# Storing spectra in DRAM by channel and chunk, from SyncE's queue, with the first chunk in a store of its own

## The chip, the cores and the metric

The kernel runs on one core of a Trainium2 chip. The metric is the device time in microseconds (us) of one execution. The profile is of one execution on the chip. Its engines are PE (TensorE's matmuls), PEld (its weight loads), DVE (VectorE), ACT (ScalarE), POOL (GpSimd) and SP (SyncE, which only issues DMAs here). "L732" is line 732 of the kernel before.

## The reference, cut to what matters

A layer of neighbourhood attention and an MLP on four images of 56 x 56 pixels and 128 channels, then a second layer: a product with a global sum, and a spectral filter over the 3,136 tokens of each image.

```python
x = _L0_conv_ref(x, ...)                       # 7 x 7 neighbourhood attention, then an MLP
t = _to_tokens(x)                              # (4, 3136, 128)
t = t + _L1_attn_ref(_ln_t(t), ...)            # q * sum(k * v)
t = t + _L1_ffn_ref(_ln_t(t), ...)             # below
x = _from_tokens(t, x)

# _L1_ffn_ref, for each of four prefixes of the tokens, weighted and summed:
Vf   = rfft(phi, n); Uf_p = rfft(u, n); Uf_m = rfft(u * sgn, n)
out  = einsum('btkd,k,kde->bte', irfft(Vf * Uf_p), s, Mpp)
out += einsum('btkd,k,kde->bte', irfft(Vf * Uf_m) * sgn, s, Mpm)
out += sum over 3 lags of u shifted by the lag, times M_u[lag]
```

All that the change touches is how the spectra of `u` (the transform of the normalized tokens) pass through DRAM between the transform and the product with the filters.

## The kernel before, in words

**Stages.** The kernel has four stages in order of time. (1) Attention for images 0 to 3, in 28 steps an image; beside the steps of image b run the dense parts of image b-1 (`finish_image`: MLP, global sum, spectra) and the preparation of image b+1 (`start_image`, `keys`). A list of costs, the numbers that the generators yield, decides how many of these parts come after each attention step; up to `order.close()` the order of instructions on every engine is the one in which they are written. (2) After the last attention step, `finish_image(3)` alone, with the loading of the filter matrices into `mc` (`matrices`, L1015) ahead of its spectra. (3) The chunk loop, `for c in range(NCH)`, over 31 chunks of frequencies. (4) The way back to tokens.

**Spectra of an image** (`finish_image`, L686 to L734). The tokens of an image are in four pieces, j = 0 to 3, so with four images there are sixteen pieces. For each j and each of eight phases p, PE multiplies a `tab` tile of cosines and sines with transposed tokens into `px` (L708, 128 x 496). ACT, POOL and DVE add the eight `px` into the eight planes of `ab` (L716 to L730), a tile of 128 channels x 31 chunks x 8 planes x 16 values. When a j is complete, POOL's queue stores all of `ab` to `ud[j, b]` (L732): 128 rows, one per channel, of 31 x 512 = 15,872 bytes. In images 0 to 2 there is one `ab`; the sums of j+1 start from it and overwrite it in place (L729, L730), so DVE waits there until the store of j has landed. In image 3 two tiles alternate, so that j+2 waits for the store of j.

**What SP issues around it.** `waves` loads the `tab` tiles (L300): five tiles in images 0 to 2, so that four are ahead of the one in use, and ten in image 3. A new load waits until PE has used the tile whose place it takes. `residual(g)` fetches group g of the image two further on (L673, L99). SP's instructions run in the order written, and each waits for its own conditions.

**Chunks.** `fetch_tokens(c)` (L1036) loads the sixteen pieces of chunk c from `ud` into `xc`, a tile of 128 channels x 16 pieces x 128 values (512 bytes a piece). Chunk 0's load is cut in two, 12 pieces and 4, so that the first part need not wait for the last store. `tokens(c)` combines `xc` on POOL (chunk 0 on POOL and DVE) into `v`. `make(c, u)` multiplies filters `ph` with `mc` on PE into `pg` (L1088), and ACT and DVE copy it into `g` (L1104, L1106). `product(c, u)` multiplies `g` with `v` on PE into `py` (L1124), and the sums go to `yd` from SP (L1143). In the loop, PE alternates `make(c + 1, u)` and `product(c, u)`, 32 matmuls each, for u = 0 to 7. `tokens(c + 1)` is called at the top of chunk c; after `order.close()` the order is left to the scheduler, and SP issues a chunk's load two to three chunks before its product.

Of the kernel before, what the change touches and what calls it, by code (L numbers as in the profile page):

```python
# [9 lines left out]
FP = mybir.dt.float32  # L10
# [6 lines left out]
B, H, W, C = 4, 56, 56, 128  # L17
# [23 lines left out]
NP = 4  # L41
# [9 lines left out]
NCH = -(-R // FC)  # L51
SKIP = NCH * FC - R
FB = 4
CW = FC * PH * 2
# [6 lines left out]
def conv_attn_hybrid_kernel(ctx: ExitStack, tc: tile.TileContext, a: dict, out: bass.AP):  # L61
    nc = tc.nc

    cpool = ctx.enter_context(tc.tile_pool(name="const", bufs=1))
    dram = ctx.enter_context(tc.tile_pool(name="scratch", bufs=1, space=DRAM))
    xd = dram.tile([B, T, C], FP, name="xd")
    ud = dram.tile([NP, B, C, NCH * CW], FP, name="ud")
    pd = dram.tile([2 * NK, NCH * CW], FP, name="pd")

    yd = dram.tile([2, R, C + 8, C], FP, name="yd")  # L70
# [11 lines left out]
    def bank(name):  # L82
        return ps_s.tile([C, 512], FP, tag="s", name=name)
# [429 lines left out]
    def finish_image(b, own=None):  # L513
        x = xs[b]
# [161 lines left out]
        def last_steps(groups):  # L676
            for g in groups:
                recent(g)
                yield 2.3
                if g:  # L680
                    residual(g - 1)
                    yield 0.5
# [3 lines left out]
        ab = fp.tile([C, NCH, PH, 2 * FC], FP, tag="ab", name=f"ab_{b}")  # L686
        abs_of = (own.tile([C, NCH, PH, 2 * FC], FP, name="ab2") if own else ab, ab)
        for j in range(NP):
            before, ab = abs_of[(j + 1) % 2], abs_of[j % 2]
            toks = []  # L690
            for half in range(2):
                ps = ps_s.tile([L, 4, C], FP, tag="s", name=f"pt_{b}_{j}_{half}")
                for i in range(4):
                    at = off + N * j + PHASES[4 * half + i]
                    nc.tensor.matmul(
                        ps[:, i, :],
                        ut[:, at : at + PH * (L - 1) + 1 : PH],
                        ident,
                        is_transpose=True,
                        start=True,  # L700
                        stop=True,
                    )
                toks.append(fp.tile([L, 4, C], FP, tag="tok", name=f"tok_{b}_{j}_{half}", bufs=3))
                nc.scalar.copy(toks[half], ps)  # L704
                yield 0.4
            for i, p in enumerate(PHASES):
                ps = bank(f"px_{b}_{j}_{p}")[:, :RW]
                nc.tensor.matmul(ps, toks[i // 4][:, i % 4, :], next(tab), start=True, stop=True)  # L708
                src = ps.rearrange("c (g x) -> c g x", x=2 * FC)

                s, d = ab[:, :, p % 4], ab[:, :, 4 + p % 4]
                factor = ROOT if p % 2 else 1.0
                if p >= 4 and not (own and p == 6):
                    w = fp.tile([C, NCH, 2 * FC], FP, tag="tw", name=f"w_{b}_{j}_{p}", bufs=3)
                    nc.scalar.copy(w, src)  # L715
                    nc.gpsimd.tensor_tensor(s, s, w, ALU.add)  # L716
                    if p % 2:
                        w = fp.tile([C, NCH, 2 * FC], FP, tag="tw", name=f"wr_{b}_{j}_{p}", bufs=3)
                        nc.scalar.mul(w, src, factor)
                    nc.gpsimd.tensor_tensor(d, d, w, ALU.subtract)  # L720
                elif j == 0 and p < 4:
                    nc.scalar.copy(s, src)
                    nc.scalar.mul(d, src, factor)
                elif p >= 4:
                    nc.vector.tensor_tensor(s, s, src, ALU.add)
                    nc.vector.tensor_tensor(d, d, src, ALU.subtract)
                else:
                    s0, d0 = before[:, :, p % 4], before[:, :, 4 + p % 4]
                    nc.vector.tensor_tensor(s, s0, src, ALU.add)  # L729
                    nc.vector.scalar_tensor_tensor(d, src, factor, d0, ALU.mult, ALU.add)  # L730
                yield 0.85
            nc.gpsimd.dma_start(ud[j, b], ab.rearrange("c g p x -> c (g p x)"))  # L732
            if b < B - 1:
                yield from last_steps(range(2 * j, min(2 * j + 2, NG)))  # L734

# [199 lines left out]
    for b in range(B):  # L935

        def dense():
            if b == 0:
                setup_dense()
                yield 3.0  # L940
            yield from keys(b, 1)
            if b == 0:
                setup_gates()
                yield 0.0
                yield from filters()
            if b:
                yield "image"
                yield from finish_image(b - 1)
            if b + 1 < B:
                if b == 0:  # L950
                    fetch(b + 1)
                    yield "step"
                    yield "step"
                yield from start_image(b + 1)
                yield "keys"
                yield from keys(b + 1, 0)
# [79 lines left out]
    def fetch_tokens(c):  # L1036
        n = NP * B
        x = cp.tile([C, n, CW], FP, tag="xc", name=f"xc{c}")
        src = ud.rearrange("j b c w -> c (j b) w")[:, :, CW * c : CW * (c + 1)]

        for part in (slice(n),) if c else (slice(n - B), slice(n - B, n)):
            nc.sync.dma_start(x[:, part], src[:, part])
        fetched[c] = x

    def tokens(c):


        if c:
            fetch_tokens(c)
        n, x = NP * B, fetched.pop(c)  # L1050
        y = x.rearrange("c n (p r f) -> c p r n f", r=2, f=FC)
        gp = nc.gpsimd
        of, tag, bufs = [C, 3, 2, 2, n, FC], *(("od", 1) if c else ("v", 2))
        if c == 0:
            od = cp.tile(of, FP, tag=tag, name=f"od{c}", bufs=bufs)
        v = cp.tile([C, 3, n * FC, PH], FP, tag="v", name=f"v{c}")
        w = v[:, 1:].rearrange("c r k m -> c m r k")
        ev = cp.tile([C, 4, 2, n, FC], FP, tag="od", name=f"ev{c}", bufs=1)
        evens(gp if c else nc.vector, ev, y[:, :4], w[:, :4])
        if c:  # L1060
            od = cp.tile(of, FP, tag=tag, name=f"od{c}", bufs=bufs)
        odds(gp, od, y[:, 4:])
        od = od.rearrange("c i p r n f -> c i p r (n f)")
        gp.tensor_tensor(w[:, 4:6], od[:, 0], od[:, 2], ALU.add)
        gp.tensor_tensor(w[:, 6:], od[:, 0], od[:, 2], ALU.subtract)
        gp.tensor_scalar(v[:, 0], v[:, 2], -1.0, 1.0, ALU.mult, ALU.mult)
        spectra[c] = v
# [110 lines left out]
    with tc.tile_pool(name="last", bufs=1, side="right") as own, tc.tile_pool(  # L1178
        name="weigh", bufs=1, side="right"
    ) as wp:  # L1180
        extra, due, last = matrices(wp), 0.0, finish_image(B - 1, own)
        for spent in last:
            if spent == "spectra":
                break
            due += 0.45 * (spent if spent != "step" else 0.5)
            while due >= 1:
                next(extra, None)
                due -= 1
        run(extra)


    cp = chunks.enter_context(tc.tile_pool(name="w3", bufs=2, side="right"))
    filters_of(0)
    fetch_tokens(0)
    for n, _ in enumerate(last):
        if n == 2 * NG - 3:
# [29 lines left out]
    with tc.tile_pool(name="w4", bufs=1) as wp, tc.tile_pool(  # L1226
        name="ps_t", bufs=8, space=PSUM
# [232 lines left out]
```

## Time and profile before

| what | value |
|---|---|
| runs of the kernel | 1994.88, 1998.28, 2002.96 us; median 1998.28 |
| profiled execution, its own time | 2011.3 us |
| its span, first to last instruction | 2009.5 us |
| mean granted TensorE clock | 0.966 |
| busy share of the span: PE, PEld, DVE, ACT, POOL | 94%, 60%, 60%, 51%, 45% |
| DMA moved | 223.44 MB in 183,406 packets |
| `ud` <- `ab` (L732) | 16 DMAs of 1,984 KB on POOL's queue, 8.5 us from issue to landing (median) |
| `xc` <- `ud` (L1042) | 30 DMAs of 1,024 KB, one of 768 KB, one of 256 KB, on SP's queue |

The profiled execution was some 13 us slower than the median of the runs; durations below come from it. A group's line names the line of code, the engine, the operation and its tiles, "output<-inputs". A wait is put down to the instruction that released it; "issue" means that the engine waited for nothing that the profile shows. The chain of waits follows the work that ended last back from the end of the span: 77% of it is PE, 8% issue, 6% DVE and 4% DMA.

### The profile page before, as it was taken

To read this page: it belongs to the slowest core of one execution; us is meant where nothing else is said; L and a number is where in the kernel's file an instruction comes from. 1 tells how busy PE (TensorE), PEld (TensorE's weight loads), DVE (VectorE), ACT (ScalarE), POOL (GpSimd) and SP (SyncE) were. 2 spreads that over 40 slices of the span, in tenths; PEclk is the share of its full clock that TensorE was granted. 3 is DMA by queue.
4 is the path that set the end of the run, shared out by engine and by line. 5 is a ranking of instruction groups with operands and counts; after the bars stand their busy time and mean duration, and the time that the engine had idled before them with its cause. 6 is when DMAs were issued, how large, how long until landed. Compare 5 with 4: busy or idle time off the path is not lost.

```text
span 2009.5 us, 57128 instructions
## 1 busy us (share of the span) xinstructions
PE 1881.9 (94%) x23926; PEld 1206.8 (60%) x23926; DVE 1204.3 (60%) x2749; ACT 1024.2 (51%) x2311; POOL 904.1 (45%) x1441
## 2 busy tenths in 40 slices
PE   6899999999999999999999998999999999996998
PEld 3555555565555555555565445888888888883333
DVE  3666635455544556445555765677676666674983
ACT  2566685655685656775555342555555555550000
POOL 2344321474322465222472036777877787760000
PEclk8799999899999999998999999999999999998999
DMA  4040000153000252000244539344444444439981
GB/s 114 22 141 12 1 1 1 28 193 131 1 1 1 85 189 79 1 1 1 94 157 176 189 105 308 91 123 124 129 125 113 121 132 116 115 105 386 353 317 64
DMA packets 183406, 223.44 MB, mean 111 GB/s; under 512 B 11576, under 2 KB 160121, under 8 KB 180556
## 3 DMA queue, kind: packets, MB, share of 16 engines
q1 hardware_dynamic: 169712, 160.53, 26.5%
q0 software_dynamic: 2352, 33.01, 4.1%
q10 hardware_dynamic: 11084, 26.24, 3.7%
q8 instruction: 189, 3.10, 0.6%
q14 instruction: 69, 0.57, 0.1%
HBM read 141.77 MB, written 77.97 MB: 109 GB/s over the span
## 4 chain that ended last, share of the span: by engine, by line
PE 77%; issue 8%; DVE 6%; DMA 4%; ACT 3%; POOL 2%; ACTq 0%; SPq 0%; DVEq 0%; POOLq 0%
PE pg L1088 14%; PE py L1124 13%; PE pi L1272 7%; PE px L708 5%; PE ppt L817 4%; PE pl L761 4%; PE ph L551 3%; PE pf L542 3%; PE par L644 3%; PE pav L874 2%; PE pv L837 2%; PE pk L483 2%; ACT p L788 1%; DVE p L774 1%; DMA ud<-ab 1%
## 5 line engine op out<-in xcount | busy, mean ns | idle before, releaser
L801 POOL TENSOR_SCALAR p<-p,den 112x280 f32<-112x280 f32 x448 | 216.2, 502 | 491.2 <-DVE den L799 254.3
L1106 DVE COPY g<-pg 128x512 f32<-128x512 f32 (+1 forms) x496 | 320.3, 691 | 171.2 <-PE pg L1088 171.1
L1104 ACT COPY g<-pg 128x512 f32<-128x512 f32 (+1 forms) x496 | 263.9, 584 | 236.8 <-PE pg L1088 236.8
L1088 PE MATMUL pg<-ph,mc 32*128 32x128 f32 x7936 | 300.4, 284 | 6.5 <-DVE g L1106 5.2
L1124 PE MATMUL py<-g,v 128*32 128x128 f32 x7840 | 283.0, 281 | 12.6 <-issue 12.2
L1088 PEld LDWEIGHTS pg<-ph,mc 32*128 32x128 f32 x7936 | 251.8, 187 | 48.1 <-issue 38.3
L788 ACT ACTIVATE p<-p,low 112x280 f32<-112x280 f32 x448 | 231.2, 517 | 91.9 <-DVE low L774 91.5
L1124 PEld LDWEIGHTS py<-g,v 128*32 128x32 f32 x7840 | 222.5, 152 | 46.8 <-issue 18.1
L774 DVE CUSTOM_DVE_ANT_0 p<-pl,bias 112x280 f32<-112x280 f32 x448 | 174.8, 446 | 15.9 <-PE pl L761 4.1
L824 DVE COPY pt<-ppt 120x448 f32<-120x448 f32 x112 | 69.4, 620 | 111.2 <-PE ppt L817 110.4
L817 PEld LDWEIGHTS ppt<-ident,p 112*120 112x120 f32 x896 | 100.4, 139 | 57.7 <-issue 40.1
L817 PE MATMUL ppt<-ident,p 112*120 112x112 f32 x896 | 127.3, 263 | 5.5 <-DVE middle L859 4.1
L708 PE MATMUL px<-tab,tok 98*128 98x496 f32 x256 | 118.1, 607 | 12.6 <-ACT tok L704 9.8
L716 POOL TENSOR_TENSOR ab<-ab,w 128x496 f32<-128x496 f32 x60 | 74.5, 1242 | 101.9 <-ACT w L715 58.3
L824 ACT COPY pt<-ppt 120x448 f32<-120x448 f32 x224 | 87.2, 444 | 56.3 <-PE ppt L817 56.2
L551 PE MATMUL ph<-ln_m,w_fc 128*128 128x448 f32 x224 | 103.8, 555 | 4.7 <-DVE ln_m L532 4.7
L761 PE MATMUL pl<-kt,qt 32*112 32x280 f32 x896 | 95.7, 444 | 11.6 <-ACT qt L502 6.0
L559 ACT ACTIVATE h<-ph,b_fc 128x448 f32<-128x448 f32 x112 | 69.4, 633 | 61.8 <-PE ph L551 60.3
L542 PE MATMUL pf<-h,w_fc 128*128 128x448 f32 x224 | 100.8, 540 | 0.0
L318 POOL TENSOR_TENSOR v<-ev 128x512 f32<-128x512 f32 x30 | 39.6, 1320 | 120.1 <-PE py L1124 120.0
L708 PEld LDWEIGHTS px<-tab,tok 98*128 98x128 f32 x256 | 48.2, 197 | 65.8 <-issue 41.5
L564 DVE SCALAR_TENSOR_TENSOR x<-pf,b_fc,x 128x448 f32<-128x448 f32 x28 | 19.1, 684 | 113.0 <-PE pf L542 113.0
(239 smaller groups left out, 3401.6 us busy)
## 6 DMA issues: line engine op xcount, KB each, us to landing
ring<-yd SPq DMA_DIRECT2D x64, 512.0 KB
ud<-ab POOLq DMA_DIRECT2D x16, 1984.0 KB, 8.5
xc<-ud SPq DMA_DIRECT2D x30, 1024.0 KB
tab<-in_tab SPq DMA_DIRECT2D x160, 189.9 KB
yd<-ys SPq DMA_DIRECT2D x118, 256.0 KB
mat<-in_M_phi_plus SPq DMA_DIRECT2D x16, 512.0 KB
mat<-in_M_phi_minus SPq DMA_DIRECT2D x16, 512.0 KB
x<-in_x SPq DMA_DIRECT2D x28, 224.0 KB
```

Source lines behind the costliest of these rows:

```text
L542: nc.tensor.matmul(po[:, :GT], late["w_fc2"][:, i, :], hts[g - 1][i], start=(i == 0), stop=(i == 3),)
L551: nc.tensor.matmul(ph[:, :GT], w_fc1[:, i * C : (i + 1) * C], lnm[:, g * GT : (g + 1) * GT], start=True, stop=True,)
L708: nc.tensor.matmul(ps, toks[i // 4][:, i % 4, :], next(tab), start=True, stop=True)
L761: nc.tensor.matmul(pls[h][:TQ, :KEYS], qts[b, g][hs, t * TQ : (t + 1) * TQ], kt[hs, r0 : r0 + KR, c0 : c0 + KC], start=True, stop=True,)
L774: nc.vector.tensor_tensor_reduce(out=f["p"][:, h, :], in0=f["pls"][h][:TQ, :KEYS], in1=bias[:, h, :], scale=-1.0, scalar=3.0e38, op0=ALU.a ...
L788: nc.scalar.activation(f["p"][:, h, :], f["p"][:, h, :], AF.Exp, bias=f["low"][:, h : h + 1], scale=-1.0, accum_out=f["den"][:, h : h + 1],)
L801: nc.gpsimd.tensor_scalar(f["p"][:, h, :], f["p"][:, h, :], f["den"][:, h : h + 1], 1.0, ALU.mult, ALU.mult)
L817: nc.tensor.transpose(ppt[:, i, :], of, ident[:TQ, :TQ])
L1088: nc.tensor.matmul(banks[rg][:, q, :], mc[r, 4 * u + q, :], t[r, at : at + CW], start=True, stop=True,)
L1104: nc.scalar.copy(into, src)
L1106: nc.vector.tensor_copy(into, src)
L1124: nc.tensor.matmul(py[32 * m : 32 * m + 32, f - f0, :], weights(v, 1 - r, f, slot), g[:, (2 * slot + r) * FC + f, :], start=(r == 0), stop ...
```

## The change

`ud` gets another layout. Before, a row was a channel of one piece, with all 31 chunks side by side. After, a row is a channel of all pieces: chunks 1 to 30 follow one another, and within a chunk its sixteen pieces lie side by side, 8,192 bytes together. Each row is followed by 1,024 unused values. Chunk 0 lies in a store of its own, `ud0`, one row of 8,192 bytes per channel.

The store of each j and image becomes two DMAs, both on SP's queue instead of POOL's: 128 pieces of 512 bytes to `ud0`, and 128 x 30 pieces of 512 bytes to `ud`. In SP's order they stand where the store is written, after the `tab` loads of that j and before what SP loads next. The load of a chunk becomes 128 rows of 8,192 bytes; chunk 0's is still cut in two (6,144 and 2,048 bytes a row) and reads `ud0` alone. In the built program the order of instructions on PE and DVE is the same as before, POOL's lacks the sixteen stores, four `ph` loads on ACT's queue stand a few instructions apart, and SP has the 32 stores; the rest is unchanged.

```diff
-    ud = dram.tile([NP, B, C, NCH * CW], FP, name="ud")
+    ud0 = dram.tile([C, NP * B, CW], FP, name="ud0")
+    ud = dram.tile([C, (NCH - 1) * NP * B * CW + 1024], FP, name="ud")
+    ud_of = ud[:, : (NCH - 1) * NP * B * CW].rearrange("c (g n w) -> c g n w", g=NCH - 1, w=CW)
...
-            nc.gpsimd.dma_start(ud[j, b], ab.rearrange("c g p x -> c (g p x)"))
+            spectrum = ab.rearrange("c g p x -> c g (p x)")
+            nc.sync.dma_start(ud0[:, B * j + b], spectrum[:, 0])
+            nc.sync.dma_start(ud_of[:, :, B * j + b], spectrum[:, 1:])
...
     def fetch_tokens(c):
         n = NP * B
         x = cp.tile([C, n, CW], FP, tag="xc", name=f"xc{c}")
-        src = ud.rearrange("j b c w -> c (j b) w")[:, :, CW * c : CW * (c + 1)]
+        src = ud_of[:, c - 1] if c else ud0
 
         for part in (slice(n),) if c else (slice(n - B), slice(n - B, n)):
             nc.sync.dma_start(x[:, part], src[:, part])
```

## The prediction

> **What bounds the kernel now.** I read the profile in this order: busy time by stage, the chain of work that ended last, then the stages that touch `ud`, instruction by instruction. The first view is busy time of the engines in stretches of the span. Its columns are the stretch, its length, the busy us of PE, PEld, DVE, ACT and POOL with instruction counts, then the granted clock, the DMA share and GB/s. The three lines are the spectra of image 0 beside attention, the last image's spectra, and the chunk loop.
> ```profile
> 380.00:475.00 95.00, 90.77 (x637) 56.90 (x637) 51.96 (x165) 53.82 (x145) 64.04 (x89) 0.96 0.47 159
> 1190.00:1247.00 57.00, 52.93 (x191) 30.56 (x189) 25.00 (x42) 22.45 (x43) 34.11 (x33) 0.97 0.83 282
> 1272.00:1808.00 536.00, 523.73 (x15069) 451.22 (x15064) 372.61 (x589) 287.47 (x530) 400.45 (x547) 1.00 0.44 119
> ```
> PE is the bound of the chunk loop (524 of 536 us), with POOL at 400 and DMA at 0.44. So the chunk loads can only matter where they make PE wait. They do. The timeline of one chunk (start, length, engine and line; idle time and its end in brackets):
> ```profile
> 1501.87 0.36 SPq L1042 DMA_DIRECT2D xc<-ud  x1
> ...
> 1505.61 1.12 PE L1124 MATMUL py<-g,v 128*32 128x128 f32 x32
> ...
> 1507.85 0.99 PE L1124 MATMUL py<-g,v 128*32 128x128 f32 x25
> ...
> 1509.53 0.47 PE L1124 MATMUL py<-g,v 128*32 128x128 f32 x7 [0.69 <-issue]
> ```
> PE stops in the middle of 32 like matmuls and waits for no other engine ("issue"). The same stretch in slices of 1 us:
> ```profile
> 1503.00:1504.00 1.00, 1.00 (x40) 0.88 (x36) 0.46 (x1) 0.42 (x1) 0.92 (x3) 1.00 0.49 131
> 1504.00:1505.00 1.00, 1.00 (x40) 0.83 (x35) 1.00 (x3) 0.66 (x2) 1.00 (x2) 1.00 1.11 336
> ...
> 1507.00:1508.00 1.00, 1.00 (x36) 0.88 (x34) 0.44 (x2) 0.10 (x1) 1.00 (x2) 1.00 1.08 311
> 1508.00:1509.00 1.00, 0.84 (x25) 0.59 (x23) 1.00 (x2) 0.97 (x2) 1.00 (x2) 1.00 0.59 166
> 1509.00:1510.00 1.00, 0.47 (x11) 0.32 (x11) 0.15 (x1) 0.00 (x0) 1.00 (x3) 1.00 0.07 21
> ```
> The load has the DMA engines full from about 1503 to 1508, and PE starves right after. What is missing is instructions, which the page's list of DMA queues shows to come by DMA too:
> ```profile
> q8 instruction: 189, 3.10, 0.6%
> ```
> That is packets, MB and share; 16,384 bytes a packet. In the trace's packet records these start about every 4 us, except the one that falls on a load: in the chunks from 1285 on it starts 4.5 to 5.2 us after the load's issue, when the load's last pieces have gone (1506.94 here, after 1500.15).
>
> Last, who waits for the stores: the waits around `ud`, and two lines of DVE's timeline in the last image.
> ```profile
> DVE ab L729: 17.1, 5
> ...
> DMA to landing us min/median/max: 6.6/8.5/10.4
> ```
> ```profile
> 1211.27 0.67 DVE L729 TENSOR_TENSOR ab<-ab,px 128x496 f32<-128x496 f32 x1 [2.20 <-DMA ud<-ab]
> ...
> 1221.79 0.67 DVE L729 TENSOR_TENSOR ab<-ab,px 128x496 f32<-128x496 f32 x1 [4.12 <-DMA ud<-ab]
> ```
> DVE may overwrite `ab` only when the store that reads it has landed, so a later landing is late work for DVE.
>
> **What the Trainium skill says.** "Runtime: NRT & Kernel Launch", Instruction fetch mechanics: instructions are refilled in 16 KiB blocks of 256 through a DMA queue of their own, and the cost of a block is "mostly hidden". The trace agrees on the size; hidden it is not here (0.69 us above). "DMA: Bandwidth & Descriptors", Queues, rings and completion order: a DMA engine changes queues only at packet boundaries, at most 64 descriptors. Here the fetch waited for all 128 pieces an engine had of the load, so the wait is at least as long as that says. Same page, Two DMAs through the same engine are not ordered: transfers of one queue start in order. So what SP issues after a store starts after its pieces. Same page, Latency and other measured facts: a row pitch of a large power of two slows DRAM, and 4 KiB of padding restores it. The new pitch, (30 x 16 x 128 + 1024) x 4 = 249,856 bytes, is such a padded one; no run here shows its effect, and I take no penalty.
>
> **The change, part by part.**
> *Loads (L1042).* Now 2,048 pieces of 512 bytes, 128 per engine. The packet records give 27 ns for such a piece: 3.5 us, which with 1.0 us to the first piece ends near 4.6 us after issue, as seen. After: 128 rows of 8,192 bytes, 8 per engine. This size is not in the trace; between 6,272 bytes (239 ns) and 12,544 (476 ns) on a hardware queue lies 311 ns, so 2.5 us, ending at 3.5 us. The fetch can start some 1.2 us sooner. What it is worth: loads are issued at 1284.92 and, 26 chunks on, at 1760.07, so 18.28 us a chunk. Eight undisturbed pairs of 32 `pg` and 32 `py` matmuls, 2.157 us each (1731.17 to 1733.33), are 17.25. The excess is 1.03 x 26 = 26.7 us, nearly all in the one pair after the load (3.51 us at 1727.66, 2.59 in the chunk of 1303). No such stall is much over 1.35, so 1.2 us removes nearly all: I take **24 us off**, for 27 chunks. Bounds: 0 (the wait has another cause) and 28 (all excess gone). Below zero is not excluded by the trace, as 8 KB pieces might hold an engine longer; I give that no weight of its own, since the bytes and their total time shrink.
>
> *Stores.* Sixteen DMAs of 128 rows on POOL's queue become 32 on SP's, of 128 and 3,840 pieces. POOL sheds 16 x 0.6 us; PE paces that stage, so I count nothing. Drain before: 8 x 595 ns = 4.8 us if alone. After: 240 x 27 ns = 6.5 us; 38 ns, the 95th percentile, would be 9.1. From POOL's last operation on `ab`, landing before: 0.3 + 6.6/8.5/10.4 = 6.9/8.8/10.7, the slow ones beside `tab` and `x` loads on the other queue. After: 0.45 for the small store's issue, 1.0 to the first piece, 6.5, and 0.6 to the release (sem to DVE as before) = 8.6, and no later transfer of SP's competes. So +0.5 us on a mean. It gates DVE nine times in images 0 to 2 (three turns each); attention's work lies beside it, so I count half: 9 x 0.25 = **+2.3 us**.
>
> *What SP has behind the stores.* SP now waits for POOL, and behind stand `tab` loads (L300), `x` loads (L99) and, at the end, `ph` and `xc`. In images 0 to 2 the `tab` loads needed next are already issued. But the `x` loads of groups 5 and 6 after the fourth store are due at once: PE multiplies them (L390) from 478.93. They land near 481.4 behind a store that starts at 473.7 and drains by 480.2, against about 479.8 needed: +1.6 us, for images 2 and 3, **+3.2 us**.
>
> *Last image.* POOL ends the first store's data at 1202.5. Store pieces run 1204 to 1210.5, landing 1211.3, as before (1211.27). The first `tab` load behind it, due at 1210.5, lands near 1211.8: PE +1.3. The next store's pieces follow seven or eight `tab` loads (0.58 us each at 168 packets a us) and land near 1222, as before; the `tab` behind lands at 1222.5, and PE ends this stage **1.7 us late**. Chunk 0's loads stand behind the fourth large store, but read smaller pieces and wait for the small stores alone: landed near 1243.5, against 1244.2 now, and DVE turns to them only after 1245.8. Nothing gained, nothing lost; without that cover each us would cost one.
>
> **Sum:** -24 + 2.3 + 3.2 + 1.7 = -17 us. The profiled execution took 2011.3 us (span 2009.5 and 1.8 around it), so 1994. It lies 13 us above the median of the runs, 1998.28; I carry the difference over: **1981**.
>
> **The rivals.** *A: the loads are not what holds the fetch*, or an engine's eight large pieces hold it as long, or rows are cut into short pieces after all (the change not doing what it says; 12,544-byte packets in the trace speak against). The stall stays, the costs stay: 1998 + 7 = 2005. For it: the size of packet is new. Against: the fetch starts with the load's end in every chunk.
> *B: slower.* The store's 512-byte pieces written 8 KB apart go slower than 27 ns, and SP's queue hands the delay on. Each us of drain costs about 9 x 0.5 for DVE, 2 for `x` loads and 3 for the last image, 9.5 us; so 17 us are gone at 1.8 us more drain, 35 ns a piece. At 45 ns (+4.3 us, 41 us) it gives 1981 + 41 = 2022. For: contended pieces took 38 ns. Against: the `yd` stores, also 512-byte pieces, take 27 to 34 ns.
>
> **Chances.** Forecast 0.66, A 0.20, B 0.14. Half a per cent, 10 us, is about what can be told from no change. The forecast's own range is 1970 (all 28 us, no cost) to 1991 (20 us gained, 13 lost), a little of it within 10 us; A lies within; B mostly beyond. So faster 0.64, same 0.23, slower 0.13. The range reaches to A's time: 1970 to 2004.
>
> **What will show it.** Right: chunk loads 17.3 to 17.4 us apart, no "issue" gap of PE after them, the fetch about 3.6 us after issue. L729's waits for `ud` near 17 us or a few more; PE's `px` in the last image waiting for `tab` once or twice for 1 to 2 us. Wrong: chunks still at 18.2 (A), or stores landing over 10 us after POOL's last operation and PE's px waiting for it (B).

## The result and the profile after

The changed kernel is slower, not faster: 2022.2 us (median of 4 runs, 2013.2 to 2028.0) against 1996.6 us for the kernel before beside it, ratio 1.012 (95% interval 1.0073 to 1.0167). Measured once more (experiment 12) it is 1.0137 (1.0108 to 1.0166). The forecast was 1981, range 1970 to 2004. The profiled execution took 2020.1 us with a span of 2018.3. After the change a line from `finish_image` on has a number higher by 4 to 6: L729 is now L733, L732 is L737 (small store) and L738 (large store), L1042 is L1048, L1088 is L1094, L1124 is L1130.

First the busy time by stage, image 0's spectra, the last image's, and the chunk loop; the second and third stretch are moved to where these stages now lie. The first is not, though image 0's first store stands 9.3 us earlier in it than before.
```profile
380.00:475.00 95.00, 86.67 (x576) 52.90 (x574) 44.14 (x140) 50.69 (x134) 59.76 (x81) 0.95 0.53 149
1212.00:1270.00 58.00, 53.19 (x176) 29.27 (x175) 23.31 (x39) 21.54 (x41) 29.14 (x24) 0.94 0.83 243
1301.00:1837.00 536.00, 522.57 (x15296) 453.80 (x15296) 377.97 (x596) 288.08 (x531) 400.92 (x548) 0.99 0.43 131
```
The loop does what was forecast: in 536 us PE now gets through 15,296 matmuls, before 15,069. In image 0's spectra PE gets through 576 in 95 us (580 when the stretch is moved by 9 us), before 637, and its busy time falls from 90.8 to 86.7 us.

The gain first. The timeline of one chunk (start, length, engine and line) around its load:
```profile
1523.00 0.33 SPq L1048 DMA_DIRECT2D xc<-ud  x1
1523.49 1.17 PE L1094 MATMUL pg<-ph,mc 32*128 32x128 f32 x32
1524.60 1.12 PE L1130 MATMUL py<-g,v 128*32 128x128 f32 x32
1525.65 1.17 PE L1094 MATMUL pg<-ph,mc 32*128 32x128 f32 x32
1526.75 1.12 PE L1130 MATMUL py<-g,v 128*32 128x128 f32 x32
1527.81 1.25 PE L1094 MATMUL pg<-ph,mc 32*128 32x128 f32 x32
1528.98 1.12 PE L1130 MATMUL py<-g,v 128*32 128x128 f32 x32
```
The 32 matmuls run through, without the "issue" gap. Loads are issued at 1313.3 and, 26 chunks on, at 1769.3: 17.54 us a chunk, before 18.28.

Then the loss. The timeline of image 0 at its first store, SP's queue and what waits on DVE:
```profile
394.06 1.22 POOL L724 TENSOR_TENSOR ab<-ab,wr 128x496 f32<-128x496 f32 x1
...
395.31 0.35 SPq L737 DMA_DIRECT2D ud<-ab  x1
...
395.71 0.43 SPq L738 DMA_DIRECT2D ud<-ab  x1
...
396.18 4.77 SPq L103 DMA_DIRECT2D x<-in_x  x1
...
401.05 12.26 SPq L304 DMA_DIRECT2D tab<-in_tab  x8
...
404.98 0.67 DVE L733 TENSOR_TENSOR ab<-ab,px 128x496 f32<-128x496 f32 x1 [5.49 <-DMA ud<-ab]
...
406.38 0.73 PE L767 MATMUL pl<-kt,qt 32*112 32x280 f32 x4 [0.32 <-DVE ab L734]
```
DVE may write `ab` 9.7 us after POOL's last operation on it (395.28). It stands idle for 5.49 us, and attention's own next matmul (`pl`) waits 0.32 us for it; longer waits follow. In the kernel before, the same write came 7.6 us after POOL's last operation (404.34), and `px`, not the store, released it:
```profile
411.92 0.67 DVE L729 TENSOR_TENSOR ab<-ab,px 128x496 f32<-128x496 f32 x1 [3.21 <-PE px L708]
```
SP's next issue after the large store takes 4.77 us in place of 0.3 to 0.4. Who waited for `ud`, in total and times:
```profile
  DVE ab L733: 37.3, 8
  POOL od L327: 19.0, 1
  DVE ev L316: 2.8, 1
```
Before, DVE waited 17.1 us in five places and POOL 13.4 us once. The chain of waits now runs through the DMAs of image 0 (start, length, what; most of it left out):
```profile
395.71 9.15 DMA ud<-ab
...
418.18 10.29 DMA ud<-ab
...
452.49 7.51 DMA tab<-in_tab
...
480.47 5.58 DMA x<-in_x
486.09 1.86 PE xm_a L394 x2
```
The store itself is on it twice, then a `tab` load and an `x` load that stand behind a store.

The two traces by stretch, cut at store and load issues (the stretch up to the first store, which the change doesn't touch, is 9.3 us shorter in the changed kernel's profiled execution; I leave it out). A *turn* is the time from one store of an image to its next.

| stretch | before, us | after, us | difference |
|---|---|---|---|
| nine turns, images 0 to 2 | 206.0 | 229.2 | +23.2 |
| fourth store to the first of the next image, three times | 592.5 | 599.9 | +7.4 |
| last image, first to fourth store | 27.4 | 30.8 | +3.4 |
| fourth store to the load of chunk 4 | 54.7 | 58.1 | +3.4 |
| 26 chunks | 475.2 | 456.0 | -19.2 |

### The profile page after: what moved, and what is told of

It is laid out like the page before. It is cut to its first block, busy times and chain, and to the rows that moved or that the text cites. A ratio compares the mean times of both kernels' runs of the same rounds, so it can differ in the third digit from the quotient of the medians.

```text
span 2018.3 us, 57154 instructions
## 1 busy us (share of the span) xinstructions
PE 1881.7 (93%) x23926; PEld 1205.6 (60%) x23926; DVE 1201.7 (60%) x2749; ACT 1023.4 (51%) x2311; POOL 893.3 (44%) x1425
## 3 DMA queue, kind: packets, MB, share of 16 engines
q1 hardware_dynamic: 174320, 193.03, 30.7%
## 4 chain that ended last, share of the span: by engine, by line
PE 72%; DMA 8%; issue 7%; DVE 6%; ACT 3%; POOL 2%; SPq 0%; ACTq 0%; DVEq 0%; POOLq 0%
PE pg L1094 14%; PE py L1130 13%; PE pi L1278 7%; PE ppt L823 4%; PE px L712 4%; PE pl L767 3%; PE ph L555 3%; PE pf L546 3%; DMA ud<-ab 3%; PE pav L880 2%; PE pv L843 2%; PE par L648 2%; DVE p L780 2%; PE pk L487 1%; DMA tab<-in_tab 1%
## 5 line engine op out<-in xcount | busy, mean ns | idle before, releaser
L1094 PE MATMUL pg<-ph,mc 32*128 32x128 f32 x7936 | 297.5, 284 | 8.2 <-DVE g L1112 8.1
L1130 PE MATMUL py<-g,v 128*32 128x128 f32 x7840 | 278.1, 281 | 3.0 <-issue 2.5
L1094 PEld LDWEIGHTS pg<-ph,mc 32*128 32x128 f32 x7936 | 249.8, 187 | 48.6 <-issue 36.2
L1130 PEld LDWEIGHTS py<-g,v 128*32 128x32 f32 x7840 | 220.9, 152 | 34.0 <-issue 5.2
L712 PE MATMUL px<-tab,tok 98*128 98x496 f32 x256 | 123.9, 628 | 18.6 <-ACT tok L708 10.1
L880 PE MATMUL pav<-pt,v 120*32 120x112 f32 x1792 | 88.0, 268 | 0.0
```

The lines of the kernel that those rows point to most:

```text
L1094: nc.tensor.matmul(banks[rg][:, q, :], mc[r, 4 * u + q, :], t[r, at : at + CW], start=True, stop=True,)
L1130: nc.tensor.matmul(py[32 * m : 32 * m + 32, f - f0, :], weights(v, 1 - r, f, slot), g[:, (2 * slot + r) * FC + f, :], start=(r == 0), stop ...
```

## The experiments

**Theory:** the loop has its gain, and the loss is the later landing of stores in short pieces, which holds DVE at `ab`, with loads behind them as a second term. **Rivals:** SP's queue order alone costs it; or short pieces cost by themselves wherever they stand. Each ratio is to the kernel before, timed beside it. In the table below, *gate* is the mean time from POOL's last operation on `ab` to DVE's next write of it, over nine turns, whether the store or `px` ends it; *next* is the sum of the three stretches to the next image.

| kernel | ratio, 95% | gate, us | nine turns | next | us a chunk |
|---|---|---|---|---|---|
| before (its profile) | 1 | 9.3 | 206.0 | 592.5 | 18.28 |
| changed (its profile) | 1.012 (1.007-1.017) | 11.1 | 229.2 | 599.9 | 17.54 |
| 1 only the loads | 0.986 (0.984-0.989) | 9.4 | 205.1 | 589.2 | 17.51 |
| 2 old rows, SP stores | 1.004 (1.002-1.005) | 8.7 | 203.6 | 591.1 | 18.34 |
| 3 new layout, POOL stores | 1.021 (1.018-1.024) | 14.0 | 261.3 | 588.5 | 17.60 |
| 4 new layout, ACT stores | 1.020 (1.017-1.023) | 11.4 | 224.6 | 617.3 | 17.54 |
| 5 x loads first | 1.007 (1.005-1.010) | 11.0 | 227.1 | 584.8 | 17.53 |
| 6 old rows, stored twice | 1.048 (1.046-1.051) | 13.8 | 262.6 | 613.9 | 18.08 |
| 7 load in four | 0.989 (0.987-0.991) | 9.1 | 204.5 | 586.9 | 17.52 |
| 8 load in two | 0.999 (0.997-1.000) | 9.3 | 203.9 | 588.5 | 18.25 |
| 9 load in eight | 0.989 (0.986-0.991) | 9.4 | 204.9 | 586.2 | 17.38 |
| 10 half the store | 0.986 (0.984-0.988) | 8.5 | 202.2 | 586.0 | 17.57 |
| 11 no pad | 1.017 (1.014-1.019) | 11.5 | 236.4 | 600.7 | 17.56 |
| 12 changed, again | 1.014 (1.011-1.017) | 11.1 | 230.8 | 601.4 | 17.55 |
| 13 x loads first, again | 1.009 (1.006-1.012) | 11.0 | 228.5 | 586.6 | 17.54 |
| 14 no pad, again | 1.015 (1.012-1.018) | 11.4 | 233.0 | 599.8 | 17.51 |

**1. Only the loads change.** The kernel before with
```diff
-        src = ud.rearrange("j b c w -> c (j b) w")[:, :, CW * c : CW * (c + 1)]
+        src = ud[c % NP, c // NP % B, :, : NP * B * CW].rearrange("c (n w) -> c n w", w=CW)
```


> The kernel before, with one thing changed: each chunk's load reads 128 rows of 8,192 bytes side by side out of the old store's layout (the numbers in them are another chunk's, so the output is not the reference's); layout and queue of the stores stay. Theory (chunk loop gains, spectra lose): chunk loads 17.5 us apart in place of 18.28, so 26 x 0.75 = 19 to 20 us faster than before, ratio about 0.990, and the spectra of images 0 to 3 as in the kernel before. Rival (the shorter interval hangs on the new store too, for example on its padded pitch): interval stays near 18.2, ratio 0.998 to 1.002.


Measured 0.986, chunks 17.51 us apart. The loop's gain is real and needs nothing of the new stores. (The ratio holds a few us that are not the loop's: chunk 0's load no longer reads the last store, and POOL waits for it 9.0 us in place of 13.4.)

**2. The store of before, from SP.** `nc.gpsimd.dma_start(ud[j, b], ...)` becomes `nc.sync.dma_start`.


> The kernel before, with its store of 128 rows of 15,872 bytes issued by SyncE in place of GpSimd; layout and chunk loads stay. Theory (the loss comes from 3,968 pieces a store, which fill SP's queue, so that the loads behind are issued 5 to 7 us late and DVE's ab comes free later): 128 rows drain in 4.8 us and don't block SP, so at most 0 to 8 us slower, ratio 1.000 to 1.004. Rival (it is the order on SP alone: tab and x loads stand behind a store that waits for POOL, whatever its pieces): 20 us or more slower, ratio 1.010 or more.


Measured 1.004. So the queue's order alone is not the loss: the nine turns are 2 us shorter than before, since rows on SP land a little sooner. What it costs lies at the end, in the last image (31.3 us against 27.4) and ahead of the loop. DVE hardly waits for the stores here:
```profile
  DVE ab L729: 6.9, 2
```

**3 and 4. The new layout from other queues.** Both stores with `nc.gpsimd` or `nc.scalar` in place of `nc.sync`.


> The changed kernel, with both stores of a spectrum issued by GpSimd (software queue) as before the change; layout and chunk loads as changed. Theory (half of the loss is loads behind the store on SP, half the later landing): tab and x loads are issued on time again, the landing stays at 10 us or more after POOL's last operation, DVE still waits over 35 us for ab; chunk loop 17.5 us a chunk; 10 to 20 us faster than the changed kernel, ratio to before 1.000 to 1.005. Rival (pieces alone cost it, wherever they are issued): 2015 to 2025 us, ratio 1.010 or more; GpSimd may also spend long on writing 4,096 descriptors, which would show as POOL idle time after each store.

> The changed kernel, with both stores issued by ScalarE on its own hardware queue in place of SyncE; layout and chunk loads as changed. Theory (loads behind the store on SP): SP issues tab and x loads on time (0.4 us an issue, not 4.8), PE's xm_a of groups 5 and 6 runs through; but ACT now waits for POOL's last operation at each store, with evictions behind it, 1 to 5 us each; net 0 to 15 us faster than the changed kernel, ratio to before 1.003 to 1.012. Rival (landing alone): no difference to the changed kernel beyond 5 us, or slower by ACT's waits.


Both miss: 1.021 and 1.020, slower than from SP. Neither queue helps. From POOL the `x` and `tab` loads are on time ("next" 588.5), but the pieces land later still, POOL's two issues take 0.6 and 1.6 us, and DVE waits twice as long as in the changed kernel:
```profile
  DVE ab L733: 77.1, 10
```
The turns are 55 us longer than before for it. From ACT DVE waits for the stores only 16.9 us, in four places; the gate of 11.4 is long because in the third turn of each image (13.5 to 14.2 us) `px` ends it, which comes late behind ACT. The turns are 5 us shorter than from SP, but "next" is 25 us longer than before, and the last image takes 42.7 us in place of 27.4. Here ACT's own next DMA issue is held behind the store, and its copies and squares for PE stand behind that issue:
```profile
473.05 0.36 ACTq L737 DMA_DIRECT2D ud<-ab  x1
473.46 1.06 ACTq L738 DMA_DIRECT2D ud<-ab  x1
474.62 0.58 ACT L673 COPY xf<-pf 112x512 f32<-112x512 f32 x1 [4.75 <-POOL p L807]
477.04 5.02 ACTq L674 DMA_DIRECT2D xd<-xf  x1
...
482.15 0.58 ACT L673 COPY xf<-pf 112x512 f32<-112x512 f32 x1 [6.95 <-PE xm_a L394]
...
482.79 1.02 PE L394 MATMUL xm_a<-x,center 128*128 128x448 f32 x2 [0.96 <-ACT xf L673]
```
The last copy is put down to PE's `xm_a`, but ACT had been busy issuing until 482.06. So the expectation that half of the loss goes once the stores leave SP's queue was wrong: to ACT the held issue moves with the store, and from POOL the landing is later still. The two do show the terms apart. From POOL, with no load of SP held, the turns alone are longer; from ACT, with shorter waits at `ab`, most of the loss lies outside the turns.

**6. Landing alone.** The kernel before with SP's rows of 15,872 bytes stored twice, the second time to a scratch `ud2`.
```diff
-            nc.gpsimd.dma_start(ud[j, b], ab.rearrange("c g p x -> c (g p x)"))
+            nc.sync.dma_start(ud[j, b], ab.rearrange("c g p x -> c (g p x)"))
+            nc.sync.dma_start(ud2[j, b], ab.rearrange("c g p x -> c (g p x)"))
```


> The kernel before, with the store of 128 rows of 15,872 bytes issued by SyncE, and issued a second time into a scratch of its own: no short pieces, but DVE gets ab back only when 256 rows have gone, 4.8 us later. Theory (what costs is the landing that gates DVE, not the number of pieces): DVE's first write to ab comes 12 to 15 us after POOL's last operation in place of 7.5 to 10, each turn between stores is 5 to 8 us longer, 15 to 20 us an image, some 45 to 60 us in all, ratio to before 1.025 to 1.035. Rival (short pieces cost by themselves, through SP's blocked issue or held instruction fetches, and half of a later landing is hidden by attention as the prediction had it): 1.010 to 1.015.


Measured 1.048, more than expected, with not one short piece in the stores. The nine turns are 59 us longer than in experiment 2. PE waits 22.8 us for DVE's writes of `ab`, and the loads behind the second store come late too: 11.6 us for `x` and 16.0 for `tab`, part of it within the turns. In this timeline SP's next issue is hardly held (0.86 us), and DVE is:
```profile
399.18 0.35 SPq L733 DMA_DIRECT2D ud<-ab  x1
399.58 0.43 SPq L734 DMA_DIRECT2D ud<-ab  x1
400.11 0.86 SPq L100 DMA_DIRECT2D x<-in_x  x1
...
411.92 0.67 DVE L730 TENSOR_TENSOR ab<-ab,px 128x496 f32<-128x496 f32 x1 [8.56 <-DMA ud<-ab]
```
So a late landing costs without short pieces and without SP's slow issue. Here some late `tab` loads are mixed in; in experiment 3 PE waits for none in images 0 to 2. The two together show the first term.

**10. Half the pieces.** The changed kernel storing 15 of the 30 chunks in `ud`, and reading them twice.
```diff
-            nc.sync.dma_start(ud_of[:, :, B * j + b], spectrum[:, 1:])
+            nc.sync.dma_start(ud_of[:, :15, B * j + b], spectrum[:, 1:16])
-        src = ud_of[:, c - 1] if c else ud0
+        src = ud_of[:, (c - 1) % 15] if c else ud0
```


> The changed kernel, storing only chunks 1 to 15 beside chunk 0 (1,920 short pieces in the large store in place of 3,840) and reading those twice over for chunks 16 to 30, so that the output is not the reference's. Queue, layout, pieces and all 27 loads of the loop stay. Theory (landing gates DVE): the large store lands some 4 us sooner, DVE's first write comes 6 to 8 us after POOL's last operation, turns are back at 68 us an image, loads behind the store are 4 us less late; only the chunk loop's gain of 20 us is left, ratio 0.989 to 0.993. Rival (short pieces on SyncE cost by themselves: blocked issue, held fetches): half of the loss stays, ratio 0.998 to 1.004.


Measured 0.986, better than expected. With the same layout, queue and kind of piece, but the last piece 5.6 us after issue in place of 10.4, the whole loss is gone: DVE no longer appears among those who wait for `ud`, and it finds `ab` free when its `px` is there. SP's next issue takes 0.71 us here, so this run takes away both terms:
```profile
402.10 0.35 SPq L737 DMA_DIRECT2D ud<-ab  x1
402.51 0.43 SPq L738 DMA_DIRECT2D ud<-ab  x1
402.98 0.71 SPq L103 DMA_DIRECT2D x<-in_x  x1
...
409.60 0.67 DVE L733 TENSOR_TENSOR ab<-ab,px 128x496 f32<-128x496 f32 x1 [3.21 <-PE px L712]
```

**5, 12, 13. x loads ahead of the fourth store.** In images 0 and 1 the fourth store is issued after `residual(NG - 1)`, which issues the last `x` loads; then the same again beside the changed kernel itself.
```diff
+            if j == NP - 1 and b + 2 < B:
+                late_store = spectrum
+            else:
                 nc.sync.dma_start(ud0[:, B * j + b], spectrum[:, 0])
                 nc.sync.dma_start(ud_of[:, :, B * j + b], spectrum[:, 1:])
...
         residual(NG - 1)
+        if b + 2 < B:
+            nc.sync.dma_start(ud0[:, B * (NP - 1) + b], late_store[:, 0])
+            nc.sync.dma_start(ud_of[:, :, B * (NP - 1) + b], late_store[:, 1:])
```


> The changed kernel, with one thing moved: in images 0 and 1 the fourth spectrum is stored only after SyncE has issued the x loads of all groups of the image two ahead. Theory (after the fourth store PE's xm_a of the next image waits for x loads that stand behind 3,840 pieces): the time from the fourth store of image 0 to the first of image 1 falls from 230 to about 222 us, and by 2 us for image 1, PE's xm_a no longer waits for x; the turns between the stores of one image stay at 77 us an image; ratio to before 1.006 to 1.009. Rival (the turns alone matter, or x loads come late for lack of DMA bandwidth wherever they stand): no difference to the changed kernel, 1.010 or more.

> The changed kernel as it is, beside the two runs that differ from it in one thing each. Theory: ratio to before 1.012 to 1.016 on this chip, 36 to 40 us above the kernels that have only the loop's gain (0.986 to 0.989 less their own differences). Rival (the loss is no larger than the first comparison's lower bound): 1.005 to 1.009.

> The changed kernel with the fourth store of images 0 and 1 behind the x loads, again, now beside the changed kernel. Theory (x loads behind the fourth store cost 10 to 15 us): 0.005 to 0.0075 less in ratio than the changed kernel of the same call. Rival (x loads behind the store are hidden, and the shorter time in the first profile was that of its fastest execution alone): less than 0.003 apart.


Measured 1.007 the first time, and on one chip 1.009 (median 2014.1 us) against 1.014 (2026.3) for the changed kernel: 12 us between the medians. The intervals just overlap (1.006 to 1.012, 1.011 to 1.017), but both pairs of traces put the difference in one place, "next": 584.8 against 599.9, and 586.6 against 601.4, 15 us each time. The turns hardly move. In the changed kernel PE's `xm_a` waits at 484.1:
```profile
473.34 8.27 SPq L103 DMA_DIRECT2D x<-in_x  x2
...
484.08 1.39 PE L394 MATMUL xm_a<-x,center 128*128 128x448 f32 x2 [2.70 <-DMA x<-in_x]
```
and with the loads first it runs through (x at 474.08, the store behind it):
```profile
474.08 0.35 SPq L103 DMA_DIRECT2D x<-in_x  x1
474.53 0.38 SPq L750 DMA_DIRECT2D ud<-ab  x1
...
482.36 2.52 PE L394 MATMUL xm_a<-x,center 128*128 128x448 f32 x6
```

**7, 8, 9. The gain without the new stores.** The kernel before with the load of a chunk cut by spectra (4, 2 and 8 parts); stores and layout stay.
```diff
-        for part in (slice(n),) if c else (slice(n - B), slice(n - B, n)):
+        for part in [slice(i, i + n // 4) for i in range(0, n, n // 4)] if c else (slice(n - B), slice(n - B, n)):
```


> The kernel before, with each chunk's load issued as four DMAs of 4 spectra each (32 pieces of 512 bytes an engine) in place of one; layout and stores stay. Theory (an instruction fetch waits for the pieces of the DMA that it falls on): if the engines turn to the fetch between two DMAs of one queue, it waits a quarter as long, chunks are 17.4 to 17.6 us apart and the ratio is 0.988 to 0.991, without any cost in the stores. Rival (the fetch waits until the queue is empty, however it is cut): 18.3 us apart, ratio 0.998 to 1.002.

> The kernel before, with each chunk's load issued as two DMAs of 8 spectra each. Theory (as for four): half of the wait goes, chunks about 17.5 to 17.9 us apart, ratio 0.990 to 0.995. Rival (the fetch waits until the queue is empty): 18.3 us apart, ratio 0.998 to 1.002.

> The kernel before, with each chunk's load issued as eight DMAs of 2 spectra each (16 pieces of 512 bytes an engine). Theory (what counts is how many pieces of one DMA stand at an engine when a fetch comes: 128 and 64 an engine gave 18.28 and 18.25 us a chunk, 32 gave 17.52): no stall is left to remove, so 17.4 to 17.6 us a chunk and a ratio of 0.987 to 0.991, as with four. Rival (the gain of four came from spreading the load over SyncE's issue time, 0.36 us each): eight take 2.9 us to issue, the last pieces come later, chunk loads delay the yd and ring traffic of the same queue, and PE or DVE waits for xc: 17.6 us or more, ratio 0.991 or more.


Four and eight parts give 0.989 each, faster than both kernels and not to be told apart; two parts give nothing. The group of `py` matmuls shows it (busy us, mean ns, then idle time ahead of it and its cause), first with two parts:
```profile
L1124 PE MATMUL py<-g,v 128*32 128x128 f32 x7840 | 282.1, 281 | 13.7 <-issue 13.2
```
then with four:
```profile
L1124 PE MATMUL py<-g,v 128*32 128x128 f32 x7840 | 275.8, 281 | 3.0 <-issue 2.7
```
From the packet records: the instruction fetch that falls on the load starts, on a mean, 4.98 us after the load's issue in the kernel before, 4.92 with two parts, 3.84 with four and 2.80 with eight; the last 512-byte piece of a load starts at 4.95, 5.04, 5.13 and 6.33. So with four parts the fetch gets in between the pieces. The expectation for two parts was wrong: if the engines turned to the fetch at the boundary of two DMAs, two parts would have helped too. Nor does the figure that the prediction took from the Trainium skill, "DMA: Bandwidth & Descriptors", Queues, rings and completion order, at most 64 descriptors before an engine changes queues, mark the step: 64 pieces an engine held the fetch as long as 128, and 32 did not. SP issues two parts in 0.98 us, four in 2.02 and eight in 4.86, so the parts' spacing may count as much as their size; the runs don't tell these apart.

**11 and 14. The pad.** `ud` without `+ 1024`.


> The changed kernel without the 1,024 numbers at the end of a channel's row (pitch 245,760 bytes in place of 249,856). Theory (the drain is set by the number of pieces, at about 30 ns each): same landing and same time as the changed kernel, ratio to before 1.009 to 1.015. Rival (the pitch sets how fast pieces go, one way or the other): pieces take 27 ns or less, or 35 ns or more, and the time moves by 15 us or more.

> The changed kernel without the 1,024 unused numbers of a row, again, now beside the changed kernel. Theory (the pad does nothing, since pieces took 30.2 ns without it and 30.4 with it): within 0.003 in ratio of the changed kernel of the same call. Rival (the pad saves something in these stores): 0.003 to 0.008 more than the changed kernel.


Measured 1.017, a little above the range expected, and beside the changed kernel 1.015 against 1.014. Pieces take 30.1 to 30.2 ns without the pad and 30.4 with it. It does nothing that these runs can tell, as the prediction took it. But the prediction read its source wrongly in calling the new pitch a padded one: the row without the pad is 245,760 bytes, not a power of two.

## Why the prediction was wrong

**Loads, -24: right in place, near in size, wrong in two inputs.** The loop gains 19.2 us. A row of 8,192 bytes takes 391 ns, not the 311 interpolated between the sizes of another queue, so the load's last row starts 4.4 us after issue, while before the last piece started at 4.95 (the forecast had 3.5 and 4.6). The fetch starts after 4.37 us, not 3.6, and takes 0.96 us in place of 1.19, so it ends at 5.3 us instead of 6.2. Those 0.8 us were enough for 0.74 of the 1.03 us a chunk. That the gain came so near was in part luck: the fetch starts 0.6 us sooner and not 1.2, and the 0.23 us by which it is itself shorter was not in the step.

**Stores, +2.3: the step that failed.** It was the product of three numbers. Nine turns stands. "+0.5 us on a mean" measured +1.8 (gate 9.3 to 11.1). The step's own figures did not give it either: 8.6 after lies below the 8.8 in the middle of the range before. And 8.6 was too small. Pieces took 30.4 ns and not 27, which is 0.8 us on 240; 27 is the middle value of the load's pieces before, but their mean is 30.7, and a sum needs the mean. The step also let no other transfer compete, while the last piece started 10.4 us after the small store's issue, where 248 pieces at 30.4 ns from the first at 0.8 would end at 8.4. In that time rows of 2,048 bytes on ACT's queue took 0.3 to 1.9 us of each DMA engine, and in three of the nine stores `x` rows on SP's own queue another 0.8 to 1.0. Last, "attention's work lies beside it, so I count half" is wrong beyond a small slack:

| from, to | gate, us | mean turn, us | turn per us of gate |
|---|---|---|---|
| half the store (10), before | 8.5 to 9.3 | 22.5 to 22.9 | 0.5 |
| before, changed | 9.3 to 11.1 | 22.9 to 25.5 | 1.4 |
| changed, from POOL (3) | 11.1 to 14.0 | 25.5 to 29.0 | 1.2 |

Up to a gate of 8.5 us, where `px` and not the store ends DVE's wait in all nine turns, the landing is covered. From 9.3 on, each us lengthens a turn by more than 1 us; counted from experiment 10 the slope is 1.2 for the changed kernel and for POOL's stores alike. The first reason is DVE's order. It takes its instructions in order, and behind the held write stand attention's `den` and `pt`, for which PE and POOL wait. So at image 0's second store:
```profile
428.59 0.67 DVE L733 TENSOR_TENSOR ab<-ab,px 128x496 f32<-128x496 f32 x1 [5.30 <-DMA ud<-ab]
...
429.77 0.17 DVE L805 RECIPROCAL den<-den 112x4 f32<-112x4 f32 x1
...
429.99 1.28 PE L767 MATMUL pl<-kt,qt 32*112 32x280 f32 x4 [1.72 <-DVE den L805]
```
Attention is not beside the wait; it is queued behind it. From 395 to 1190 us PE's `pl` waits 7.4 us for `den`, before 0.7, and 13.7 with stores from POOL.

The second reason is PE's clock. The same place by stretch (length, busy PE, PEld, DVE, ACT and POOL, then the granted clock):
```profile
428.30:430.00 1.70, 0.01 (x1) 0.04 (x2) 1.41 (x4) 0.00 (x0) 0.59 (x1) 0.99 0.99 375
430.00:436.80 6.80, 6.80 (x36) 3.76 (x37) 3.90 (x14) 2.16 (x8) 4.05 (x7) 0.50 0.31 78
436.80:445.00 8.20, 8.20 (x60) 4.85 (x59) 5.42 (x17) 5.52 (x15) 7.28 (x7) 1.00 0.38 112
```
PE stands still for 1.7 us and then has half the clock for 6.8 us. In the nine turns the changed kernel has five such stretches, 27 us together, the kernel before one of 3.4 us, and stores from POOL twelve, 72 us. Each of the eighteen begins within a wait of PE of 1.1 to 4.8 us or at most 1.5 us after its end; not every such wait has one. Experiment 10, with short waits, is back at one of 3.4 us. That the wait brings on the lower clock is read from this order in time; no run tests it apart. Over the nine turns PE is idle 13.1 us longer than before (10.2 to 23.3), and busy 10.4 us longer with the same instructions (195.6 to 206.0): per us of gate, 0.8 us of waiting and 0.6 of slower matmuls. Of the waiting, 2.7 us are for `tab`. The term is then 9 x 1.8 x 1.4 = 23 us; the slope is taken from the same stretches, so this only says what the three factors should have been.

**SP behind the stores, +3.2: too small, and a step left out.** `tab` was said to be "already issued". Only four of the next eight tiles are ahead, and PE does wait for the fifth (2.65 us at 460.1, chain line 452.49). For `x`, two images at 1.6 us each were priced; leaving it out saves 15 us in the traces and 12 between medians. The +7.4 is against the profile of before; experiments 1, 7, 8 and 9, which have its stores, take 586.2 to 589.2 us for "next", 11 to 14 less than the changed kernel. I had the start of the store and its drain, but not that SP's own next issue is held for 4.7 to 7.0 us behind 3,840 pieces, nor that PE's late `xm_a` opens the next image's chain.

**Last image, +1.7:** 3.4 us against the profile of before; but experiments 1, 7 and 9, whose last image is that of before, have 29.4 to 29.7 us there, and the changed kernel 30.8 and (12) 32.3, so it is between 1 and 3 us: right in size.

**Chunk 0, nothing lost:** 3.4 us lost. SP's `ph` loads stand between the last large store and `xc`, and four of them took 10.0 us to issue (1256.3 to 1266.3), so `xc` was issued at 1266.6 and POOL waited 19.0 us for it, before 13.4. (How much of the 3.4 us is the store's is not shown: experiments 7 and 9, with the stores of before, take 57.7 us for this stretch, nearly the 58.1 of the changed kernel.) The step had followed `xc` past the store, but not past what else the store holds up.

With these terms the sum is -19.2 + 23.2 + 7.4 + 3.4 + 3.4 = +18 us in place of -17, inside the measured interval of 1.0073 to 1.0167 (15 to 33 us). **Rival B** named much of the right mechanism, a longer drain, and its sign came true, stores landing over 10 us after POOL's last operation. Its reason did not: pieces were at 30 ns, under its break-even of 35. But the drain took 9.5 us from the first piece to the last in place of 6.5, well past its break-even of 1.8 us more; at its own price that is 1981 + 29 = 2010. That its 2022, worked out for 45 ns, is the time measured is luck. It used the same sensitivity of 9.5 us for each us of drain, and that was what had to be questioned: by the slopes it is 9 x 1.4 for DVE alone. The views named ahead worked: L733's wait for `ud` is 37.3 us and not "17 us or a few more".

**What stays open:** why two DMAs of 64 pieces an engine hold the fetch as long as one of 128, while four of 32 don't; whether PE's waits bring on the half clock behind them. A second `ab` in images 0 to 2, which should take the gate away, was not tried.

## What to carry to other kernels

A store that reads a buffer which is soon overwritten has a deadline; ask how much slack the landing has left, because up to there a slower store is free and beyond it every us was paid in full here, by all that stands behind the waiting instruction on its engine, and once more in matmuls at half the clock after PE's waits. Moving short pieces from the reading side to the writing side did not pay here, because the writer could not wait. Where the aim is only to let another transfer in (here instruction fetches), first try to cut the same load into four DMAs: it gave 1.1% with nothing to pay back.

## What the runs showed of the hardware

- Behind a store of 3,840 pieces of 512 bytes the next DMA issue of the same engine takes 4.7 to 7.0 us (SP) or 5.0 (ACT, at 477.0) in place of 0.3 to 0.4; behind 256 rows of 15,872 bytes mostly 0.86.
- Rows of 8,192 bytes took 391 ns on a hardware queue in the loop, where the line between 239 ns for 6,272 bytes and 476 for 12,544 on another gives 311.
- GpSimd's queue carried the same pieces in packets of 4,096 bytes (230 ns each), so short pieces are bundled there; DVE still got `ab` back 3 us later than from SP.
- In the nine turns PE's granted clock is 0.5 for 27 us of the changed kernel and for 3.4 of the kernel before, in stretches of 3.4 or 6.8 us, each beginning within a wait of PE of over 1 us or shortly after it.
